# One load moved from SyncE's queue to ScalarE's, ahead of the row of parameters

## The chip, the cores and the metric

The kernel runs on one core of a Trainium2 chip. The metric is device time in microseconds (us) of one execution. Before the change it is 157.71 us, the median of 3 runs (157.62 to 158.26).

Engines are called by the profile's names: PE (TensorE, matrix products), PEld (its weight loads), DVE (VectorE), ACT (ScalarE), POOL (GpSimd), SP (SyncE, which here only issues DMAs). ACTq and SPq are the instruction queues of ACT and SP where they issue DMAs. Each engine works through its own queue in order.

## The reference

One block of a gated network on x (4 batches, 512 tokens, 512 features, float32), with a context of 4 x 512 tokens of 128 features:

```python
# attention part: W is [1, 256], ctx is [4, 512, 128]
si = ctx @ W[0, :128];  sj = ctx @ W[0, 128:]              # [4, 512] each
xij = sigmoid(si[:, :, None] + sj[:, None, :] + b)
x = x + tanh(g_xattn) * (0.6 * xij + 0.4 * layernorm(x))
# feed-forward part, all three products with quantized operands
h = layernorm(x)
x = x + tanh(g_ffn) * bitlinear(silu(bitlinear(h, w1)) * bitlinear(h, w2), w3)
```

`bitlinear(x, w)` normalizes x by its root mean square, rounds it to 8 bits with a scale per token, rounds w to -1, 0 or 1 after division by the mean of |w|, and multiplies. w1 and w2 are [1408, 512], w3 is [512, 1408].

## The kernel before

The 2048 tokens are 16 tiles of 128 tokens (4 tiles a batch). The context comes in transposed, 128 features on the partitions, 512 tokens of one batch in a block of 256 KB (`ctx_0` to `ctx_3`). x comes in tiles of 128 x 512 (256 KB).

The order of the work is written out by hand in `ORDER`, a list of steps; a table `STEPS` maps each step's name to a function, a loop at the end calls them in that order, and each engine gets its instructions in that order. Steps that matter here:

- `x0`, `x3`, ...: load a tile of x, on SP's queue (L133). `ctx0` to `ctx3`: load a block of the context, on SP's queue, by `load_ctx` (L139). `w1.0` and so on: load a part of a weight, on SP's queue (L144 for w1 and w2, L150 and L155 for w3).
- Ahead of the list: ACT's queue loads the row of attention weights `w_att` (1 KB, on one partition, into the tile `row`, L109), then the three scalars g_xattn, b_att and g_ffn into the same tile (`load_param`, L113). Then ACT runs one activation on the tile `warm` (L171), in front of which its function table is loaded.
- PE runs three filler products (`keep_busy`, L180, tile `idle`), then two products that turn the row into a column and into 128 equal rows (L185, L186, tile `bc`); ACT copies these to `wc` (L188).
- `bp1`, `up1`, `bp0`, `up0`: spread a scalar over the partitions on PE (L196) and take it up on ACT (L202, L204).
- `pi0`, `pj0`: the scores of batch 0 from `wc` and `ctx_0`, on PE (L315, L322). `si0` and `th`: bias and tanh on ACT (L327, L338). `st`, `at`: statistics of x and the gated sum, on DVE (L345, L366).
- `wu4`, `wu13`: 4 or 13 more filler products. `pi1`, `pj1`, `pi2` and so on: scores of the other batches.
- `A1.0a` ... `A1.4v`: sums of |w1| over parts, on ACT (a) or DVE (v). `tot1`: their total over the partitions, on PE (L248). `M1`: mean and its inverse, on DVE (L253 to L256). `R`, `C`: rounding and clipping of a weight (L264 to L269). `G`, `U`: the products with w1 and w2 (L459). `D`: the product with w3 (L526).

PE's queue therefore begins: three fillers, bc, bp1, bp0, pi0, pj0, pi1, four fillers, bp2, pj1, thirteen fillers, pi2, tot1. SP's queue begins: x0, ctx0, x3, x2, x1, ctx1, four parts of w1, ctx2, ctx3, four parts of w2.

Of the kernel before, what the change touches and what calls it, by code (L numbers as in the profile page):

```python
# [30 lines left out]
PACK, WORD = 4, F32  # L31

ORDER = """
x0 ctx0 x3 x2 x1 ctx1 w1.0 w1.1 w1.2 w1.3 ctx2 ctx3 w2.0 w2.1 w2.2 w2.3 x10 w3.0 x4 x6 x8 w3.1 w3.2
x14 x12 st0 bp1 up1 cg cc st3 bp0 up0 pi0 si0 st2 pj0 th2 st1 la2 th0 la0 th1 pi1 lb2v at2 si1 lb0v
at0 ce0v at1 ce1v am0 an0 th3 at3 am1 an1 A1.0a A1.1a A1.2a wu4 bp2 pj1 up2 wu13 pi2 A1.3v pjs1 sq1
A1.4v si2 ce3p sq0 am3 tot1 M1 ce2p r1p r0p pt1 un1a R1.2v pt0 un0v R1.3a am2 an3 pi3 si3 an2 C1.3v
C1.2v A2.0a th7 pj2 R1.0p C1.0v A2.1a wu4 G0.0 R1.1p A2.2v A2.3a C1.1v A2.4v G1.0 G1.1 st10 tot2 M2
R2.0v G0.1 r2v sq3 sq2 r3p G0.2 G0.3 dq0 C2.0v R2.1p st11 st5 C2.1v pjs2 R2.2a C2.2v pt3 pj3 SI0
# [23 lines left out]
def flamingo_gated_kernel(  # L63
# [16 lines left out]
    C = ctx_t.shape[0]  # L80
# [12 lines left out]
    act, dve, pool, pe, sp = nc.scalar, nc.vector, nc.gpsimd, nc.tensor, nc.sync  # L93
# [12 lines left out]


    row = const.tile([1, 2 * C + 3], F32, name="row")
    act.dma_start(row[:, : 2 * C], w_att)  # L109

    def load_param(i):
        src = (b_att, g_x, g_f)[i]
        act.dma_start(row[:, 2 * C + i : 2 * C + i + 1], src.rearrange("(o n) -> o n", o=1))  # L113
# [24 lines left out]
    def load_ctx(eng, b):  # L138
        eng.dma_start(ctxs[b], ctx_t[:, b * S : (b + 1) * S])  # L139

    def load_w(eng, i, k):
# [3 lines left out]
        else:  # L145
# [8 lines left out]
            if f1 > full:  # L154
# [2 lines left out]
                    w3t[HF:, :].rearrange("(p j) d -> p j d", j=REST),  # L157
                )

    for i in (1, 0, 2):  # L160
        load_param(i)

# [140 lines left out]
    am1 = const.tile(NTT, F32, name="am1")  # L303
# [315 lines left out]
```

## Time and profile before

| what | value |
|---|---|
| median of 3 runs | 157.71 us |
| the profiled execution, its own time | 157.83 us |
| its span, first to last instruction | 156.1 us |
| mean granted TensorE clock | 0.989 |
| PE busy | 146.2 us (94% of the span) |
| DVE busy | 126.9 us (81%) |
| ACT busy | 118.6 us (76%) |
| POOL busy | 97.4 us (62%) |
| loaded and stored | 18.21 MB |

The span is what the profile sees; the time of the execution has some 1.7 us around it. Busy shares are means over the whole span, which has a load stage, a long stretch in which PE is full, and a tail, and they say little of the first microseconds, where the change lies. For these one reads the timeline (each line: start, duration, engine, source line, operation, tiles written and read, how many in a row, and the idle time before with what ended it) and the chain of waits (the work that ended last, followed back from the end). A row of the windows view gives, for one stretch of time, its length, the busy time and number of instructions of PE, PEld, DVE, ACT and POOL, the granted clock, the share of the DMA engines and the GB/s. A row of the waits gives who waited for whom, the total in us, how often, and the longest.

### The profile page before, as it was taken

Reading aid. Unit: us, or ns where it says so; the run is one execution under the profiler, and the core shown is the slowest. Engines: PE = TensorE matmul, PEld = TensorE weight load, DVE = VectorE, ACT = ScalarE, POOL = GpSimd, SP = SyncE. Lnnn points to the kernel's source line nnn. Section 1 sums busy time; section 2 is a strip of 40 time slices with the busy share of each in tenths; the row PEclk is TensorE's granted clock in tenths of the full one; section 3 lists DMA queues with packets and bytes.
Section 4 is the critical chain, followed back from the end, with each engine's and each line's share of the span. In section 5 each row is a group of like instructions: output and inputs, shape, how many; then the busy total and the mean of one; then the engine's idle time right before and its main releaser. Section 6 shows DMA issues by size and latency. Waiting matters only on the chain.

```text
span 156.1 us, 2167 instructions
## 1 busy us (share of the span) xinstructions
PE 146.2 (94%) x704; PEld 75.4 (48%) x704; DVE 126.9 (81%) x216; ACT 118.6 (76%) x164; POOL 97.4 (62%) x161
## 2 busy tenths in 40 slices
PE   5999969979999999999999999999999999999980
PEld 2853643535554545555455454545554545555330
DVE  1679599999999999999999999959699296748621
ACT  3269499999799999997999879689979583737300
POOL 6241569782366886589959888889998962130400
PEclk9999995999999999999999999999999999999999
DMA  4799999996000000000000000100600321010162
GB/s 118 278 425 412 432 411 421 422 404 249 1 0 0 6 0 0 0 0 0 0 4 0 0 0 0 69 4 0 247 24 0 123 79 70 1 67 0 64 249 90
DMA packets 6690, 18.21 MB, mean 117 GB/s; under 512 B 663, under 2 KB 664, under 8 KB 6424
## 3 DMA queue, kind: packets, MB, share of 16 engines
q1 hardware_dynamic: 6672, 18.09, 29.4%
q8 instruction: 5, 0.08, 0.2%
q14 instruction: 5, 0.04, 0.1%
q10 hardware_dynamic: 8, 0.00, 0.0%
HBM read 13.89 MB, written 4.19 MB: 116 GB/s over the span
## 4 chain that ended last, share of the span: by engine, by line
PE 68%; DVE 21%; ACT 3%; POOL 3%; issue 1%; DVEq 0%; POOLq 0%; ACTq 0%
PE pg L459 19%; PE pu L459 18%; PE po L526 15%; PE idle L180 5%; DVE hs L471 5%; DVE f_am L483 5%; PE pj L322 3%; PE pi L315 3%; DVE x L366 2%; PE qp L419 2%; DVE x L531 2%; DVE am L388 2%; ACT junk L396 1%; DVE q L411 1%; PE pt L419 1%
## 5 line engine op out<-in xcount | busy, mean ns | idle before, releaser
L459 PEld LDWEIGHTS <-ht 128*128 128x128 f16 x384 | 37.7, 99 | 38.5 <-issue 3.5
L459 PE MATMUL pu<-w2q,ht 128*128 128x512 f16 (+1 forms) x192 | 40.4, 362 | 1.1 <-DVE w2q L269 1.1
L459 PE MATMUL pg<-w1q,ht 128*128 128x512 f16 (+1 forms) x192 | 41.1, 367 | 0.0
L526 PE MATMUL po<-w3q,qt 128*128 128x512 f16 x176 | 39.4, 379 | 0.7 <-ACT ht L427 0.4
L471 DVE SCALAR_TENSOR_TENSOR hs<-pu,a,hs 128x1408 f32<-128x1408 f32 x16 | 26.8, 1676 | 6.3 <-PE pu L459 2.4
L427 ACT ACTIVATE qt<-qp 128x1536 f16<-128x1536 int8 x14 | 20.2, 1448 | 12.9 <-PE qp L419 12.7
L526 PEld LDWEIGHTS <-qt 128*128 128x128 f16 x176 | 17.2, 98 | 20.1 <-issue 1.0
L467 ACT ACTIVATE hs<-pg,a 128x1408 f32<-128x1408 f32 x16 | 22.8, 1426 | 4.5 <-POOL a L406 2.4
L483 DVE TENSOR_REDUCE f_am<-hs 128x1 f32<-128x1409 f32 x16 | 25.7, 1609 | 0.1
L491 ACT ACTIVATE junk<-hs 128x1408 bf16<-128x1408 f32 x16 | 22.0, 1375 | 0.1
L500 POOL TENSOR_SCALAR q<-hs,f_qs 128x1024 int8<-128x1024 f32 (+1 forms) x22 | 19.2, 888 | 1.1 <-DVE f_qs L488 0.6
L531 DVE SCALAR_TENSOR_TENSOR x<-po,f_dq,x 128x512 f32<-128x512 f32 x16 | 11.9, 746 | 9.7 <-PE po L526 8.4
L345 DVE BATCH_NORM_STATS2 st<-x 128x6 f32<-128x512 f32 x16 | 10.8, 675 | 3.1 <-DMA x<-in_x_dram 3.1
L382 POOL TENSOR_SCALAR th_all<-x,ysum 128x512 f32<-128x512 f32 x9 | 6.8, 761 | 10.1 <-DVE x L366 6.6
L366 DVE SCALAR_TENSOR_TENSOR x<-x,sc,th_all 128x512 f32<-128x512 f32 x16 | 12.3, 788 | 0.7 <-ACT th_all L338 0.3
L411 POOL TENSOR_SCALAR q<-th_all,qs 128x512 int8<-128x512 f32 x15 | 10.3, 689 | 3.3 <-PE pt L419 1.4
L374 POOL TENSOR_SCALAR x<-x,c_sig,sh 128x512 f32<-128x512 f32 x14 | 11.6, 833 | 0.1
L516 POOL TENSOR_SCALAR f_w<-f_ss,kap 128x2 f32<-128x2 f32 (+1 forms) x9 | 2.4, 268 | 14.2 <-ACT junk L491 13.6
L388 DVE TENSOR_REDUCE am<-th_all 128x1 f32<-128x513 f32 x16 | 10.8, 676 | 0.0
L180 PE MATMUL idle<-ones 128*128 128x512 f16 x24 | 9.0, 534 | 1.8 <-POOL ones L175 1.8
L396 ACT ACTIVATE junk<-th_all 128x512 bf16<-128x512 f32 x16 | 10.1, 628 | 0.7
L427 ACT ACTIVATE ht<-pt 128x512 f16<-128x512 int8 x15 | 8.8, 589 | 1.9 <-PE pt L419 1.8
(94 smaller groups left out, 182.1 us busy)
## 6 DMA issues: line engine op xcount, KB each, us to landing
out_dram<-x SPq DMA_DIRECT2D x16, 256.0 KB, 2.3
x<-in_x_dram SPq DMA_DIRECT2D x6, 512.0 KB, 13.1
hs<-in_w1t_dram SPq DMA_DIRECT2D x4, 704.0 KB, 6.7
hs<-in_w2t_dram SPq DMA_DIRECT2D x4, 704.0 KB, 11.6
w3f<-in_w3t_dram SPq DMA_DIRECT2D x2, 1024.0 KB, 14.9
x<-in_x_dram SPq DMA_DIRECT2D x4, 256.0 KB, 5.1
ctx<-in_ctx_t_dram SPq DMA_DIRECT2D x4, 256.0 KB, 7.3
w3f<-in_w3t_dram SPq DMA_DIRECT2D x1, 768.0 KB
```

The costliest lines, as they stand in the source:

```text
L180: pe.matmul(idle[:, :512], ones16[:, :P], ones16, start=True, stop=True)
L366: dve.scalar_tensor_tensor(xt(n), xt(n), col(sc, n), ths[n], ALU.mult, ALU.add, accum_out=col(ysum, n))
L388: dve.tensor_reduce(col(am1, n), th_all[:, th_slot[n], : D + 1], AX.X, ALU.max, apply_absolute_value=True)
L427: act.activation(dst, src, AF.Copy)
L459: pe.matmul(gus[tag, n][:, c0 : c0 + cn], hts[n][:, kk, :], wq[:, kk, c0 : c0 + cn], start=(kk == 0), stop=(kk == ND - 1),)
L467: act.activation(tts[n], gus.pop(("pg", n))[:, :H], AF.Silu, scale=col(a1, n))
L471: dve.scalar_tensor_tensor(tts[n], gus.pop(("pu", n))[:, :H], col(a1, n), tts[n], ALU.mult, ALU.mult)
L483: dve.tensor_reduce(col(f_am, n), hs[:, t_slot[n], : H + 1], AX.X, ALU.max, apply_absolute_value=True)
L491: act.activation(junk[:, :H], tts[n], AF.Square, accum_out=col(f_ss, n))
L500: eng.tensor_scalar(dst, src, col(f_qs, n), 127.0, ALU.mult, ALU.mult)
L526: pe.matmul(po[:, :D], qt[:, f, :], w3q[:, f, :], start=(f == 0), stop=(f == NH - 1))
L531: dve.scalar_tensor_tensor(xt(n), pos.pop(n)[:, :D], col(f_dq, n), xt(n), ALU.mult, ALU.add)
```

## The change

The step `ctx0` is taken out of `ORDER`, so SP's queue goes from x0 straight to x3. In its place ACT's queue loads the first block of the context, by the same `load_ctx`, as its first DMA; the load of `w_att` now comes behind it, then the three scalars as before. Sizes, tiles and all other steps stay.

```diff
 ORDER = """
-x0 ctx0 x3 x2 x1 ctx1 w1.0 w1.1 w1.2 w1.3 ctx2 ctx3 w2.0 w2.1 w2.2 w2.3 x10 w3.0 x4 x6 x8 w3.1 w3.2
+x0 x3 x2 x1 ctx1 w1.0 w1.1 w1.2 w1.3 ctx2 ctx3 w2.0 w2.1 w2.2 w2.3 x10 w3.0 x4 x6 x8 w3.1 w3.2 x14
...
     row = const.tile([1, 2 * C + 3], F32, name="row")
-    act.dma_start(row[:, : 2 * C], w_att)
 
     def load_param(i):
...
+    load_ctx(act, 0)
+    act.dma_start(row[:, : 2 * C], w_att)
     for i in (1, 0, 2):
         load_param(i)
```

More of the change, by code (lines that the diff above doesn't have):

```diff
@@ L33 @@
 ORDER = """
-x0 ctx0 x3 x2 x1 ctx1 w1.0 w1.1 w1.2 w1.3 ctx2 ctx3 w2.0 w2.1 w2.2 w2.3 x10 w3.0 x4 x6 x8 w3.1 w3.2
-x14 x12 st0 bp1 up1 cg cc st3 bp0 up0 pi0 si0 st2 pj0 th2 st1 la2 th0 la0 th1 pi1 lb2v at2 si1 lb0v
-at0 ce0v at1 ce1v am0 an0 th3 at3 am1 an1 A1.0a A1.1a A1.2a wu4 bp2 pj1 up2 wu13 pi2 A1.3v pjs1 sq1
+x0 x3 x2 x1 ctx1 w1.0 w1.1 w1.2 w1.3 ctx2 ctx3 w2.0 w2.1 w2.2 w2.3 x10 w3.0 x4 x6 x8 w3.1 w3.2 x14
+x12 st0 bp1 up1 cg cc st3 bp0 up0 pi0 si0 st2 pj0 th2 st1 la2 th0 la0 th1 pi1 lb2v at2 si1 lb0v at0
+ce0v at1 ce1v am0 an0 th3 at3 am1 an1 A1.0a A1.1a A1.2a wu4 bp2 pj1 up2 wu13 pi2 A1.3v pjs1 sq1
 A1.4v si2 ce3p sq0 am3 tot1 M1 ce2p r1p r0p pt1 un1a R1.2v pt0 un0v R1.3a am2 an3 pi3 si3 an2 C1.3v
```

## The prediction

> **What bounds the kernel now.** I read the page first, for which engine fills which stretch, then the chain of waits, for what the first 20 us hang on, then the timeline of that stretch, then the waits of DVE and of the SP queue.
>
> The page's 40 slices (3.9 us each) have the granted clock and the DMA rate:
>
> ```profile
> PEclk9999995999999999999999999999999999999999
> DMA  4799999996000000000000000100600321010162
> GB/s 118 278 425 412 432 411 421 422 404 249 1 0 0 6 0 0 0 0 0 0 4 0 0 0 0 69 4 0 247 24 0 123 79 70 1 67 0 64 249 90
> ```
>
> The loads stream at about 420 GB/s from 8 us to 35 us; the first two slices are well below that. The chain of waits (start us, us, what) begins so:
>
> ```profile
> 1.82 1.46 PE idle L180 x3
> 3.28 0.51 PE bc L185 x2
> 3.80 0.65 PE bc L186 x2
> 4.45 0.02 issue
> 4.47 0.29 ACT wc L188
> 4.76 0.04 issue
> 4.80 0.58 PE spread L196 x2
> 5.38 0.10 issue
> 5.49 1.84 PE pi L315 x8
> 7.32 1.92 PE pj L322 x2
> ...
> 14.98 3.62 PE idle L180 x13
> 18.60 0.80 PE pi L315 x8
> ```
>
> See that PE never stands for a DMA here: the row's first matmul (L185) starts when the three fillers end, and everything up to 18.6 us is one unbroken queue on PE. DVE's waits between 8 and 36 us say what this queue holds up:
>
> ```profile
> DVE mean L253 <- PE tot L248: 1.7, 1, 1.7
> ```
>
> DVE stands 1.7 us, until 19.65, for the total of w1, which sits on PE behind that queue; its own last input for it was done at 17.4. From 19.65 to 28.0 DVE works without a gap (M1, rounding, clipping, M2), PE then waits 1.1 us for w2q (L269, 33.6), and from 33.6 PE is full. So a delay of PE's first instructions is a delay of M1, and I see no cover for it behind M1.
>
> The timeline of the start (start us, us, what):
>
> ```profile
> 0.72 0.51 ACTq L109 DMA_DIRECT2D row<-in_w_att_dram  x1
> 0.72 0.20 POOL masks.py:197 MEMSET ident<- 128x128 f32 x1 [0.29 <-POOLq L599]
> 0.72 0.38 SPq L133 DMA_DIRECT2D x<-in_x_dram  x1
> ...
> 1.16 0.42 SPq L139 DMA_DIRECT2D ctx<-in_ctx_t_dram  x1
> ...
> 1.27 0.21 ACTq L113 DMA_DIRECT2D row<-in_g_xattn_dram  x1
> ```
>
> The trace's records of semaphores and packets, which the page only sums up, say when these landed: row 1.96, x0 3.36, g_x 3.42, b 4.05, g_f 4.23, ctx0 5.35, x3 6.70. What PE wants of them: row at 3.21 (slack 1.25), g_x at 4.23 for bp1 (0.8), b at 4.80 for bp0 (0.75), ctx0 at about 5.3 for pi0, which starts at 5.46, 0.11 after ctx0 landed. So ctx0 costs 0.1 us at most today. Its landing is late for a reason: the windows view has
>
> ```profile
> 3.50:5.00 1.50, 1.35 (x7) 1.26 (x7) 0.87 (x3) 0.48 (x3) 0.00 (x0) 1.00 0.26 71
> ```
>
> 71 GB/s between 3.5 and 5.0 us, after 269 in the 1.5 us before, with ctx0 and x3 both issued. I don't know what stalls there.
>
> **The change, part by part.**
>
> *SP loses one issue.* 0.42 us of SP (1.16 to 1.58); x3 and x2 are issued that much earlier. Worth nothing on the chain: the only wait for these in the stretch is DVE's 0.7 us for x3 at 6.7, and DVE has 1.7 us to spare before M1. Were that cover gone, it would be worth 0.4 us.
>
> *ACT gains one issue in front of four.* Nearest rows: 0.33 to 0.42 for a ctx block on SP, 0.51 for ACT's first issue. I take 0.45, so row, g_x, b, g_f and the table load (2.09, 1.28 us) all start 0.4 to 0.5 later. ACT's first consumer, wc, starts at 4.47 after 0.9 us of idling, so the table load is covered; without that idling it would cost the 0.45.
>
> *The row now queues behind 256 KB.* This is the term that counts. The row has one partition, and its records are one 1024-byte packet (0.044 us) and one 4-byte one, on one DMA engine. In the trace of before, that engine worked off the small and the large transfers in turn: row at 1.62, eight x0 packets of 2 KB, g_x at 2.88, eight ctx0 packets until 3.53, then b and g_f at 3.54 and 3.56. So 2-KB packets ahead do delay a 4-byte one: g_x took 2.2 us from issue to landing, against 1.24 for the row. After the change row, g_x, b and g_f stand in ACT's own queue behind ctx0's eight packets, with x0's eight running beside them. Those 16 packets took until 3.53 before; I take the same. Row packet at 3.55, landing 0.3 (row) to 0.5 (g_x, b) later: 3.95. PE's L185 then starts at about 4.0 instead of 3.21: +0.8. Bounds: if ACT's packets all go ahead of x0's, ctx0's share ends near 2.9 (as x0's did) and the row lands at 3.3, +0.1; if the row is caught in the stalled stretch and lands only when ctx0 did, 5.35, it is +2.2. Landings of g_x and b right behind the row (4.1 to 4.2) stay within their wanted times, which move too (5.0 and 5.6). From the +0.8 the 0.1 us that pi0 stood for ctx0 comes off: **+0.7 at pi0**.
>
> The Trainium skill, page "DMA: Bandwidth & Descriptors", section "Issuing engines are not separate DMA queues", speaks against the change: DMAs issued from several engines run on the same 16 DMA engines and interleave, so a second issuer saves only the sequencer's time. By that rule the gain is the 0.42 us of SP above, which nothing waits for, and the sum stays positive; the order in which the trace shows engine 0 serving both queues agrees.
>
> *SP's later issues.* The SP queue waits for earlier transfers:
>
> ```profile
> SPq L144 <- DMA ctx<-in_ctx_t_dram: 1.2, 1, 1.2
> SPq L599 <- PEq L599: 0.7, 1, 0.7
> SPq L139 <- DMA x<-in_x_dram: 0.6, 2, 0.3
> ```
>
> The trace has eight landing semaphores in turn; a ninth transfer waits for the first. Today x1 (2.59) waits for the row, ctx1 (3.38) for x0, w1.0 for g_x, w1.1 (5.37) for ctx0. With ctx0 first in line, x1 probably waits for ctx0 or x0: issued at 3.4 to 3.9, some 1 us later, with ctx1, w1.0 and the rest queued behind it. Ahead of them x0, ctx0, x3 and x2 are 1 MB, 2.5 us at 420 GB/s, so the engines have work until about 4.8, and x1's first packet comes about 1 us after its issue (x0: 0.72 to 1.75). I cost it at nothing. Cover: pi1 starts at 8.71 and ctx1 landed at 8.60; with PE 0.7 later ctx1 may land at 9.3. If it comes later, each us costs PE a us.
>
> *What of +0.7 reaches the end.* The next thing on PE that isn't paid in work is the clock. Four fillers at 10.60 took 1.87 us (0.43 apart); of the 13 from 14.78 the first four start 0.43 apart and the rest 0.216. The clock records show full rate from 16.49 to 23.32, half to 26.73, then full again: steps of 3.41 us. If the step at 16.49 stays where it is, PE's fillers begin at 15.48, only 2.4 of them run slow instead of 4, and the queue's end moves by 0.35 and not by 0.7. If the step moves with the work or by chance, all 0.7 pass. I take the middle, **+0.5**. The skill's page "TensorE: Matmul & The Clock Gate", Part 1, says that the window is free-running and doesn't restart with the kernel; by it the 0.35 of one execution is not a rule, and the mean would be 0.7. The 3.41 us spacing agrees with its figure.
>
> Sum: 157.83 (the profiled execution; span 156.1 and 1.7 around it) + 0.5 = 158.3; it stands 0.12 above the median 157.71, which gives **158.2**.
>
> **The rivals.**
>
> *No difference: the row is not late.* The engines may serve ctx0 on ACT first and the row at 2.9. Then pi0 gains its 0.1: 157.6. Against: x0 and ctx0 start in the same 0.1 us and the first packets take 0.26 to 0.4 us each.
>
> *Slower, clearly: the stall takes the row.* If the row's read is caught in what held the engines at 71 GB/s, it lands between 4.7 and 5.35, PE starts 1.5 to 2.2 later and, with half to all of it passed on, the time is 158.5 to 159.8; middle 159.2. It decides from a landing of about 4.4 on. For it: ctx0 itself took 4.2 us. Against: b and g_f passed at 3.54.
>
> *Slower by the clock.* If the window that ends at 16.49 isn't busy enough any more, the nine fast fillers cost 0.21 more each: +1.9, 159.6 or so. PE's wait of 0.8 lies at 3.3, far from it.
>
> *Faster: the stall disappears.* With ctx0 and x0 abreast the 1.5 us at 71 GB/s may be filled, and the whole stream come up to 1.2 us earlier. The one place where the chain touches data in the first 36 us is ctx0 (0.1), so a gain needs a DMA wait that the view hides, or a clock step to its favour: 156.9 at best guess. Against: DVE had A1.3v's data at 15.49 and still stood for PE, and w3.1 landed at 35.11 for a use at 35.94.
>
> **How the numbers follow.** 0.5% (0.79 us) is about what a measurement of this kernel can tell. Row late by 0.3 to 1.1: 0.50, giving 157.9 to 158.8, of which 0.19 lies above 158.50 (all 0.7 or more passed on, or the row later than I take it) and 0.31 below. No difference: 0.15. Stall takes the row: 0.18, all above. Clock: 0.07, above. Faster: 0.10, below 156.92. So slower 0.19 + 0.18 + 0.07 = 0.44, same 0.31 + 0.15 = 0.46, faster 0.10. The range goes from 157.1 (leaving out most of the faster case) to 159.5 (leaving out half of the clock's and the top of the stall's).
>
> **What would show it.** Right: ACTq issues ctx0 at 0.72 and the row at 1.2; L185 starts at about 4.0 with an idle gap on PE ended by the row's DMA; pi0 at 6.1 to 6.2 with ctx0 landed long before; DVE's wait for tot stays near 1.3 to 1.7, since its own work before it waits for pj0 and moves too, and ends at 20.0 to 20.4 instead of 19.65; everything from M1 on is shifted alike. Wrong: L185 still at 3.2, or at 5 and later; pi0 waiting for ctx0; pi1 waiting for ctx1; a clock step at another place than 16.5.

## The result, and the profile after

The changed kernel takes 158.69 us (median of 11 runs, 158.22 to 159.80) beside 157.62 us for the kernel before (11 runs, 156.65 to 158.88). The ratio is 1.0085, 95% interval 1.0057 to 1.0113: slower by 0.85%. Run again beside other kernels it was 1.0065 (1.0038 to 1.0092). A ratio leaves out a run that lies more than 1.5% above the fastest of its kernel; in all that follows this is one run of the version with fewer fillers. The profiled execution took 158.40 us, its span is 156.6 us. Code lines are one higher after the change (L185 is L186, L459 is L460), and L133, L139 and L144 are now L132, L138 and L143.

The timeline of the first five microseconds after the change, with lines left out:

```profile
0.72 0.40 ACTq L138 DMA_DIRECT2D ctx<-in_ctx_t_dram  x1
...
0.72 4.68 SPq L132 DMA_DIRECT2D x<-in_x_dram  x4
...
1.15 0.54 ACTq L160 DMA_DIRECT2D row<-in_w_att_dram  x1
...
4.85 0.55 PE L186 MATMUL bc<-ones,row 1*128 1x1 f32 x2 [1.56 <-DMA row<-in_w_att_dram]
4.91 0.69 DVE L346 BATCH_NORM_STATS2 st<-x 128x6 f32<-128x512 f32 x1 [3.91 <-DMA x<-in_x_dram]
```

PE now stands 1.56 us for the row, which landed at 4.71 (before: 1.96), and the first product of the row comes at 4.85 instead of 3.21. DVE stands for x0, too, which landed at 4.88 instead of 3.36. And ctx0, the transfer that the change puts first, landed at 5.06 instead of 5.35: issued 0.44 us earlier, it came 0.29 us earlier. The SP line says more: its four loads of x tiles take 4.68 us together, because the fourth, x1, is not issued before 5.07. The waits of SP in the first 9 us, after the change:

```profile
SPq L132 <- DMA ctx<-in_ctx_t_dram: 3.0, 1, 3.0
SPq L600 <- PEq L600: 0.7, 1, 0.7
```

So SP stood 3.0 us for ctx0. Everything behind x1 on its queue moved: ctx1 landed at 10.21 (before 8.60), the last part of w1 at 17.18 (15.49), the last of w2 at 26.45 (23.67). The chain of waits no longer begins with PE's fillers; its start, to 26 us:

```profile
...
0.72 4.34 DMA ctx<-in_ctx_t_dram
5.06 0.02 issue
5.07 0.33 SPq L132
5.40 0.04 issue
5.45 0.43 SPq L138
5.88 0.04 issue
5.92 6.01 DMA hs<-in_w1t_dram
11.94 0.02 issue
11.95 12.82 DMA hs<-in_w2t_dram
24.77 0.02 issue
24.79 1.62 DVE acc L245
...
```

It runs through ctx0's landing, SP's held issue, the weights, and into DVE's sum over a part of w2 (step A2.2v), which waits for its data. Before, no DMA stood in the first 30 us of this chain. DVE's waits between 8 and 36 us say the same in small:

```profile
DVE x L367 <- ACT th_all L339: 0.9, 1, 0.9
DVE mean L254 <- PE tot L249: 0.8, 1, 0.8
...
DVE acc L245 <- DMA hs<-in_w2t_dram: 0.3, 1, 0.3
```

The wait for w1's total, 1.7 us before, is 0.8, although M1 comes later (20.31 instead of 19.65): DVE's own work before it ended at 19.47 instead of 17.96, so later by more. M2 comes at 28.54 instead of 27.96, and from there on nothing differs: the span ends 128.1 us behind M2 in both.

### The profile page after: what moved, and what is told of

The parts are those of the page before. It is cut to its first block, busy times and chain, and to the rows that moved or that the text cites. A ratio compares the mean times of both kernels' runs of the same rounds, so it can differ in the third digit from the quotient of the medians.

```text
span 156.6 us, 2167 instructions
## 1 busy us (share of the span) xinstructions
PE 145.3 (93%) x704; PEld 75.0 (48%) x704; DVE 126.6 (81%) x216; ACT 118.4 (76%) x164; POOL 97.4 (62%) x161
## 3 DMA queue, kind: packets, MB, share of 16 engines
HBM read 13.89 MB, written 4.19 MB: 115 GB/s over the span
## 4 chain that ended last, share of the span: by engine, by line
PE 53%; DVE 24%; DMA 15%; POOL 3%; ACT 1%; issue 1%; SPq 0%; DVEq 0%; ACTq 0%
PE pu L460 18%; PE pg L460 17%; PE po L527 15%; DMA hs<-in_w2t_dram 8%; DVE hs L472 5%; DVE f_am L484 5%; DMA hs<-in_w1t_dram 4%; DMA ctx<-in_ctx_t_dram 3%; DVE x L367 2%; PE qp L420 2%; DVE x L532 2%; DVE am L389 2%; DVE acc L245 2%; DVE st L346 1%; DVE q L412 1%
## 5 line engine op out<-in xcount | busy, mean ns | idle before, releaser
L460 PEld LDWEIGHTS <-ht 128*128 128x128 f16 x384 | 37.5, 98 | 37.7 <-issue 2.2
L460 PE MATMUL pu<-w2q,ht 128*128 128x512 f16 (+1 forms) x192 | 40.4, 361 | 1.1 <-DVE w2q L270 1.1
L460 PE MATMUL pg<-w1q,ht 128*128 128x512 f16 (+1 forms) x192 | 40.3, 361 | 0.0
L181 PE MATMUL idle<-ones 128*128 128x512 f16 x24 | 8.0, 480 | 1.8 <-POOL ones L176 1.8
```

The lines of the kernel that those rows point to most:

```text
L460: pe.matmul(gus[tag, n][:, c0 : c0 + cn], hts[n][:, kk, :], wq[:, kk, c0 : c0 + cn], start=(kk == 0), stop=(kk == ND - 1),)
```

## The experiments

Two theories. *The row*: it lands late behind ctx0, PE starts late, M1 and all behind it move. *The held queue*: x1 and what stands behind it on SP wait for ctx0, so ctx1 and the weights come late. A third thing had to be watched, the step of PE's clock, whose place I couldn't predict.

This table has, for each profile, the times in us of the row's first product on PE, of pi0, of ctx1's landing, of pi1 and pj1 on PE, of the clock's step to full rate, of M1 and M2, and the span less M2. All are read from the timelines and the trace's records of landings and clock.

| kernel | row on PE | pi0 | ctx1 landed | pi1 | pj1 | clock step | M1 | M2 | span - M2 |
|---|---|---|---|---|---|---|---|---|---|
| before | 3.21 | 5.49 | 8.60 | 9.03 | 12.91 | 16.49 | 19.65 | 27.96 | 128.1 |
| before_look1 | 3.21 | 5.52 | 8.99 | 9.12 | 13.13 | 14.28 | 18.67 | 26.84 | 128.1 |
| before_look2 | 3.21 | 5.32 | 8.67 | 8.89 | 12.81 | 14.01 | 18.37 | 26.56 | 128.1 |
| after | 4.85 | 6.92 | 10.21 | 10.49 | 14.37 | 15.89 | 20.31 | 28.54 | 128.1 |
| after_again | 4.80 | 6.87 | 10.32 | 10.46 | 14.47 | 16.08 | 20.32 | 28.52 | 128.1 |
| hold_x1 | 3.21 | 5.41 | 10.38 | 10.51 | 14.52 | 17.81 | 21.11 | 29.42 | 128.0 |
| late_row_free_sp | 3.62 | 5.69 | 9.93 | 10.07 | 14.08 | 16.96 | 20.47 | 28.78 | 128.1 |
| row_ctx_par | 3.20 | 6.82 | 7.63 | 10.39 | 14.27 | 17.76 | 20.96 | 29.27 | 128.1 |
| row_on_sp | 4.37 | 6.43 | 8.67 | 10.01 | 13.89 | 15.41 | 19.61 | 27.87 | 128.1 |
| hold_row | 10.43 | 12.49 | 8.49 | 16.07 | 19.95 | 23.35 | 26.59 | 34.91 | 128.0 |
| row_par_ctx | 3.21 | 8.34 | 9.29 | 11.89 | 15.76 | 18.40 | 22.03 | 30.34 | 128.1 |
| wu8 | 3.21 | 6.82 | 9.28 | 10.37 | 14.24 | 15.68 | 19.25 | 27.58 | 128.1 |
| ctx0_first | 3.21 | 5.40 | 10.00 | 10.14 | 14.15 | 18.48 | 21.26 | 29.57 | 128.1 |
| ctx0_first_wu8 | 3.21 | 5.39 | 9.92 | 10.06 | 14.07 | 15.93 | 19.24 | 28.55 | 128.0 |

The last column is the reading that carries the rest: in fourteen profiles, over a range of 8 us, the end comes 128.0 to 128.1 us behind M2. What a change does ahead of M2 passes to the end one to one, and in none of these versions did a later load count.

**The changed kernel again.** No edit.

> The changed kernel once more, beside the next three on the same chip. Both theories take it as it was: ratio to before near 1.0085, the row's first matmul (L186) near 4.8 us, x1 issued on SP near 5.1 us.

Ratio 1.0065 (1.0038 to 1.0092); x1 issued at 5.40, the row on PE at 4.80, M1 at 20.32 as in the first profile (20.31). But M1 is not held up by the same thing. DVE's waits between 8 and 36 us, cut to one line:

```profile
DVE acc L245 <- DMA hs<-in_w1t_dram: 0.9, 1, 0.9
```

Here DVE stands 0.9 us for the last part of w1, which landed at 18.07 (17.18 in the first profile), and has no wait for PE's total of w1, which is done at 20.28; DVE turns to it at 20.32. So the held queue reaches M1 by a way that doesn't lead over PE: the landing of w1's last part and 2.25 us of DVE's work behind it. Before the change that sum would be 15.49 + 2.25 = 17.74, 1.9 us ahead of M1.

**Hold SP's queue, leave the row.** In the kernel before:

```diff
+    pool.tensor_copy(xs[0][:, 1, 0:1], wc[:, 0:1])
     for step in ORDER.split():
```

> The kernel before, with one POOL copy of a column of wc into the place of x1 ahead of its load, so that SP cannot issue x1 (nor what is queued behind it) before wc is there, about 5.0 us instead of 2.6; the row stays early. The theory that the late row costs the time expects no difference, ratio 0.998 to 1.002, with M1 at 19.6 to 19.8. The rival, that the held-up SP queue and the later load stream cost it, expects w2's last part 1 to 2 us later than 23.7, DVE or ACT waiting for w2, and a ratio of 1.004 to 1.009.

Ratio 1.0098 (1.0062 to 1.0134). The theory of the row alone falls here: the row is as early as before, pi0 starts at 5.41, and the kernel is as slow as the changed one. The waits of its first 12 us and of SP's first 8 us:

```profile
PE pi L315 <- DMA ctx<-in_ctx_t_dram: 1.3, 1, 1.3
```

```profile
SPq L133 <- POOL x L571: 2.4, 1, 2.4
```

SP stands 2.4 us, ctx1 lands at 10.38, and PE stands 1.3 us for it ahead of pi1, which starts at 10.51, where it starts in the changed kernel too (10.49). DVE's wait isn't for w2, as the expectation had it: it stands 2.4 us for w1's last part (landed at 18.10) and then 0.7 for PE's total.

**Keep the row late, free SP.** In the changed kernel:

```diff
-    def load_param(i):
+    def load_param(i, eng=act):
         src = (b_att, g_x, g_f)[i]
-        act.dma_start(row[:, 2 * C + i : 2 * C + i + 1], src.rearrange("(o n) -> o n", o=1))
+        eng.dma_start(row[:, 2 * C + i : 2 * C + i + 1], src.rearrange("(o n) -> o n", o=1))
...
+    load_param(1, sp)
     load_ctx(act, 0)
     act.dma_start(row[:, : 2 * C], w_att)
-    for i in (1, 0, 2):
+    for i in (0, 2):
         load_param(i)
```

> The changed kernel with only g_xattn's load moved to the head of SP's queue, so that x1 on SP waits for that small transfer instead of ctx0; the row still stands behind ctx0 on ACT's queue. The theory of the late row expects L186 at 4.0 to 5.0 us, as in the changed kernel, and a ratio of 1.004 to 1.009. The rival of the held-up SP queue expects a ratio of 0.998 to 1.002, since x1 is issued near 2.6 us again.

Ratio 1.0072 (1.0037 to 1.0106), but the edit did not do what it was meant to. x1 still waited for ctx0 (2.7 us on SP, issued at 5.21), and the row landed at 3.49, so PE lost only 0.4 us by it. It is a second case of a held queue with an almost punctual row: PE stands 0.6 us for ctx1 ahead of pi1 at 10.07, and DVE 1.1 us for w1's last part. It speaks against the row alone, too, and does not test what it was built for.

**Row first, then ctx0, then the scalars, on ACT.** In the changed kernel:

```diff
-    load_ctx(act, 0)
     act.dma_start(row[:, : 2 * C], w_att)
+    load_ctx(act, 0)
```

> The changed kernel with the row's load put back as ACT's first, ctx0 behind it and then the scalars: one part of the change undone, ctx0 stays on ACT's queue. Both theories expect the row to land near 2.0 us, x1 to be issued near 2.6 us again and a ratio of 0.997 to 1.002. If the two queues side by side are themselves the cost (contention of ctx0 with x0), the ratio stays above 1.004. The scalars now stand behind ctx0: if b or g_xattn lands after 5 us, pi0 starts later than 5.5 for that reason.

Ratio 1.0073 (1.0042 to 1.0104); both theories expected none. The row landed at 1.95, x1 was issued at 2.08 and ctx1 landed at 7.63, the earliest of all. But the scalars now stood behind ctx0, and the waits of the first 12 us say what that does:

```profile
PE spread L197 <- DMA row<-in_g_xattn_dram: 1.5, 1, 1.5
```

PE stands 1.5 us for g_xattn, which landed at 5.83 instead of 3.42; pi0 started at 6.82, and pi1 at 10.39 with its data there since 7.63. SP's queue was not quite free: it stood 2.1 us for ctx0 ahead of w1's first part, yet w1 landed as before (its last part at 15.45, before 15.49), and w2's third part at 23.25, 6.0 us ahead of M2. So a late start of PE alone also gives the loss. What is late need not be the row: here it is another small transfer behind ctx0. The third case of the expectation, ctx0 and x0 in each other's way, has this number too, but PE waits for neither: x0 landed at 3.22 and ctx0 at 5.65, ahead of g_xattn.

**Move only the row, behind x0 and ctx0 on SP.** In the kernel before:

```diff
-    act.dma_start(row[:, : 2 * C], w_att)
...
     for i in (1, 0, 2):
         load_param(i)
+    load_x(0, 1)
+    load_ctx(sp, 0)
+    sp.dma_start(row[:, : 2 * C], w_att)
```

with x0 and ctx0 taken out of `ORDER`.

> The kernel before, with only the row's load moved: from the head of ACT's queue to SP's queue behind x0 and ctx0. ctx0 stays on SP, and x1 waits for a small early transfer, so SP is not held. By the order in which the engine served the queues before, the row's packet comes at 3.55 us and lands at 3.9 to 4.1. The theory that PE's start sets M1 expects L185's successor (the row's first product) at 4.0 to 4.2 us, pj1 0.6 to 0.9 later than 12.9, M1 later by that or by half of it, depending on where the clock step falls, and a ratio of 1.001 to 1.007. The rival that only the held SP queue counts expects M1 unmoved and a ratio of 0.998 to 1.001.

Ratio 1.0022 (0.9997 to 1.0047). The row landed at 4.23, its product came at 4.37, PE stood 1.1 us, and pj1 was 1.0 later than before, all a little above what was expected. M1 at 19.61 is no later than in the first profile of before, because the clock's step fell at 15.41 here, ahead of the fillers (2.97 us instead of 3.82). The time moved the expected way, by 0.35 us, which the interval (0.74 at most) separates neither from none nor from much of the 1.0 us: this run doesn't decide between the theories.

**Hold the row long.** In the kernel before, the load of the row is taken from its place and issued behind a memset on POOL (the lines of q8 are moved up from below):

```diff
-    act.dma_start(row[:, : 2 * C], w_att)
...
     pool.memset(ones16, 1.0)
+    QS, q_slot = 3, itertools.count()
+    q8 = const.tile([P, QS, NQ * P], I8, name="q8")
+    pool.memset(q8[:, :, HF:], 0)
+    pool.memset(row[:, 0:1], 0.0)
+    act.dma_start(row[:, : 2 * C], w_att)
...
-    QS, q_slot = 3, itertools.count()
-    q8 = const.tile([P, QS, NQ * P], I8, name="q8")
-    pool.memset(q8[:, :, HF:], 0)
```

> The lateness of the row doubled: the kernel before, with the row's load held by a POOL memset into the row and by the landing of ctx0, so that it is issued on ACT near 5.4 us and lands near 6.7. SP's queue and ctx0 are as before. The theory of PE's start expects the row's first product near 6.8 us (3.6 later than before), pj1 near 16.4, M1 near 22.3 if the fillers all run at full clock, and a ratio of 1.014 to 1.023. The rival of the SP queue expects at most 1.003.

Ratio 1.0442 (1.0413 to 1.0471). The memset was done at 3.11; the row, whose turn it was to wait for ctx0 (landed at 5.46), was issued at 5.54, as meant, and landed not at 6.7 but at 10.29: 4.75 us for 1 KB, with the parts of w1 under way on SP's queue. PE stood 7.15 us. So the delay was twice the one intended, and it passed whole: pj1 7.0 us later, M1 6.9, M2 7.0, the span 6.9. The row's path alone can set the end, with SP's queue as before.

**ctx0 on ACT's queue behind row and scalars.** In the changed kernel:

```diff
-    load_ctx(act, 0)
     act.dma_start(row[:, : 2 * C], w_att)
     for i in (1, 0, 2):
         load_param(i)
+    load_ctx(act, 0)
```

> ctx0 on ACT's queue behind the row and the three scalars: both suspected costs of the change are gone, the move itself stays. The row lands at 2.0 us, the scalars by 3.5, ctx0 at 5.0 to 5.6, x1 is issued near 2.6 and ctx1 lands at 7.5 to 8.6. Both theories expect pi0 at 5.3 to 5.8 and a ratio of 0.997 to 1.002; if the move itself costs through two large transfers side by side, 1.004 or more.

Ratio 1.0128 (1.0099 to 1.0158), worse than the changed kernel and outside what either theory expected; by the number it is the third case, in which the move itself costs. The row and the scalars are about as early as before, and SP issues x1, ctx1 and w1 about as early. But ctx0, issued at 2.11 behind x0, x3, x2 and x1 of the other queue, landed at 8.21:

```profile
8.34 1.84 PE L316 MATMUL pi<-wc,ctx 128*128 128x1 f32 x8 [2.95 <-DMA ctx<-in_ctx_t_dram]
```

Now pi0 itself stands 2.95 us. That queue order costs more than the change did. Whether ctx0 lost this time as the fifth in line or because large transfers ran side by side, the run doesn't say.

**Fewer fillers.** In the kernel before:

```diff
-at0 ce0v at1 ce1v am0 an0 th3 at3 am1 an1 A1.0a A1.1a A1.2a wu4 bp2 pj1 up2 wu13 pi2 A1.3v pjs1 sq1
+at0 ce0v at1 ce1v am0 an0 th3 at3 am1 an1 A1.0a A1.1a A1.2a wu4 bp2 pj1 up2 wu8 pi2 A1.3v pjs1 sq1
```

> The kernel before with 8 instead of 13 filler products ahead of pi2 (wu8 for wu13); nothing else. The theory that M1's time, set by PE's queue, passes to the end one to one expects pi2, tot1 and M1 about 1.1 us earlier (M1 at 18.5 to 18.8, DVE is ready at 18.0) and a ratio of 0.991 to 0.996. If something else than M1 sets the end, the ratio stays within 0.998 to 1.002; if the clock falls to half in the stretch for want of fillers, M1 gains nothing and the ratio is 1.000 to 1.010.

Ratio 0.9919 (0.9889 to 0.9949): 156.75 us beside 158.03. This is the version that beats both kernels. In its profile ctx0 happened to land at 6.68, pi0 at 6.82, and M1 still came at 19.25 and M2 0.4 earlier than in the first profile of before. The gain is what the shortened queue ahead of M1 would give (1.1 us by five fillers at 0.216); the gain by the ratio is 1.3 us. One of its six runs took 158.93 us, at a mean granted clock of 0.978 where the others had 0.989 to 0.994; the last experiment comes back to that.

**The kernel before, profiled twice more.**

> The kernel before, unchanged, profiled again. ctx0 landed at 5.0 to 5.5 us in most profiles that leave its load alone, but at 6.7 in wu8, which has the same loads. If that landing is a matter of chance, another profile of the same kernel gives another value between 5 and 7, pi0 follows it 0.1 us behind, and the clock's step falls at another place than 16.49. If both are fixed for this kernel, 5.35 and 16.49 come back within 0.1.

> The same once more, for the same question: two values of ctx0's landing and of the clock's step beside the first profile's 5.35 and 16.49.

Times 156.72 and 156.42 us. ctx0 landed at 5.38 and 5.18 and pi0 started within 0.2 us of the first profile, so that part came back. The clock's step did not: 14.28 and 14.01 instead of 16.49. M1 came 1.0 and 1.3 us earlier by it, and the time followed. PE's part of the timeline from 12 us on, in the first profile of before, then in before_look2:

```profile
12.91 2.08 PE L322 MATMUL pj<-ctx,wc 128*128 128x512 f32 x2
14.78 3.82 PE L180 MATMUL idle<-ones 128*128 128x512 f16 x13
18.43 0.95 PE L315 MATMUL pi<-wc,ctx 128*128 128x1 f32 x8
```

```profile
12.81 1.70 PE L322 MATMUL pj<-ctx,wc 128*128 128x512 f32 x2
14.35 2.97 PE L180 MATMUL idle<-ones 128*128 128x512 f16 x13
17.16 0.95 PE L315 MATMUL pi<-wc,ctx 128*128 128x1 f32 x8
```

pj starts within 0.1 us of the same place; the thirteen fillers take 2.97 us instead of 3.82, since the step to full rate came ahead of them, and the products behind them start 1.27 us earlier. The same kernel, and as much as the change is worth. In the changed kernel's profile the step came ahead of the fillers too:

```profile
14.37 1.87 PE L323 MATMUL pj<-ctx,wc 128*128 128x512 f32 x2
16.07 2.97 PE L181 MATMUL idle<-ones 128*128 128x512 f16 x13
19.03 1.02 PE L316 MATMUL pi<-wc,ctx 128*128 128x1 f32 x8
```

So the two profiles can't be set against each other without the clock. From 14.37 against 12.91 the change has 1.46 us of lateness ahead of the fillers, and 0.60 behind them: 0.86 was given back by the fillers, which is a matter of where the step fell. Against before_look2, with the step ahead of the fillers in both, the lateness is 1.56 us at pj and 1.87 at the products. The ratio from many runs, 1.0 to 1.3 us, is the better measure of the change than any pair of profiles.

**ctx0 first, on SP's own queue.** In the kernel before, the line of `ORDER` that SP works off:

```diff
-x0 ctx0 x3 x2 x1 ctx1 w1.0 w1.1 w1.2 w1.3 ctx2 ctx3 w2.0 w2.1 w2.2 w2.3 x10 w3.0 x4 x6 x8 w3.1 w3.2
+ctx0 x0 x3 x2 x1 ctx1 w1.0 w1.1 w1.2 w1.3 ctx2 ctx3 w2.0 w2.1 w2.2 w2.3 x10 w3.0 x4 x6 x8 w3.1 w3.2
```

> The aim of the change by another way: ctx0 ahead of x0 on SP's own queue, the row first on ACT as before. ctx0 lands near 3.3 us, where x0 landed before, and x0 near 5.3. If what hurts is the row's and the scalars' place, and ctx0's own landing costs the kernel before only 0.1 us, the ratio is 0.997 to 1.001, with pi0 at 5.3 to 5.5. If ctx0's landing varies and costs the kernel before more on average, 0.992 to 0.997. If x0 is missed more than ctx0, 1.002 or more, with DVE's first gate constants behind x0.

Ratio 1.0081 (1.0051 to 1.0110). The row is as early as before (1.96), no scalar is waited for (b landed at 4.63 instead of 4.05), no queue is changed but by the exchange of two neighbours, and the time is that of the changed kernel. The wait came, though not where the expectation put it. SP's waits of the first 8 us, and PE's second start of pi in the timeline:

```profile
SPq L139 <- DMA ctx<-in_ctx_t_dram: 2.2, 1, 2.2
```

```profile
5.40 1.84 PE L315 MATMUL pi<-wc,ctx 128*128 128x1 f32 x8
7.10 2.05 PE L322 MATMUL pj<-ctx,wc 128*128 128x512 f32 x2
10.14 1.84 PE L315 MATMUL pi<-wc,ctx 128*128 128x1 f32 x8 [0.98 <-DMA ctx<-in_ctx_t_dram]
```

ctx0, issued at 0.72 as the first of its queue, landed at 5.26; as the second, at 1.16, it had landed at 5.35. The issue of ctx1, whose turn it now is to wait for ctx0 instead of x0, stands 2.2 us; ctx1 lands at 10.00 and PE stands 1.0 us for it. This is the held queue with a punctual row once more, and without a POOL instruction put in.

**ctx0 first, with fewer fillers.** Both edits:

```diff
-x0 ctx0 x3 x2 x1 ctx1 w1.0 w1.1 w1.2 w1.3 ctx2 ctx3 w2.0 w2.1 w2.2 w2.3 x10 w3.0 x4 x6 x8 w3.1 w3.2
+ctx0 x0 x3 x2 x1 ctx1 w1.0 w1.1 w1.2 w1.3 ctx2 ctx3 w2.0 w2.1 w2.2 w2.3 x10 w3.0 x4 x6 x8 w3.1 w3.2
...
-at0 ce0v at1 ce1v am0 an0 th3 at3 am1 an1 A1.0a A1.1a A1.2a wu4 bp2 pj1 up2 wu13 pi2 A1.3v pjs1 sq1
+at0 ce0v at1 ce1v am0 an0 th3 at3 am1 an1 A1.0a A1.1a A1.2a wu4 bp2 pj1 up2 wu8 pi2 A1.3v pjs1 sq1
```

> ctx0 ahead of x0 on SP and 8 fillers for 13 together. If both act on PE's queue ahead of M1 and DVE is ready at 18.0, M1 comes at 18.4 to 19.0 and the ratio is 0.987 to 0.993, the end 136.3 to 136.5 us behind M1 as in every profile so far. If the fillers are missed by the clock, M1 is at 19.5 or later.

Ratio 1.0054 (1.0015 to 1.0092): most of the gain of wu8 is gone. In the profile PE's queue did get shorter, M1 comes at 19.24 as in wu8, though here DVE has no wait for PE's total and w1's last part sets M1 (landed at 17.00, M1 2.24 later). But M2 comes 9.3 us behind it, where all other profiles have 8.2 to 8.3. DVE's waits between 8 and 36 us:

```profile
DVE acc L244 <- DMA hs<-in_w2t_dram: 1.3, 1, 1.3
```

The sum A2.2v stands 1.3 us for the third part of w2, which landed at 24.74, 3.8 us ahead of M2; in the changed kernel's profile it landed at 24.77, 3.8 ahead of M2, and DVE stood 0.3; in wu8's, where ctx0 came late by chance, at 23.80, 3.8 ahead of M2, and DVE stood 0.4. So M2 is the later of two things, M1 + 8.2 to 8.3, and the landing of that part + 3.8. With SP's queue held, the second forms a floor: 24.77 + 3.8 is 28.57, within 0.05 us of M2 of the changed kernel, and M1 + 8.2 to 8.3 comes there too. In that profile PE being earlier would be worth nothing more. The landing varies between runs, and much of the loss is something else: five of the twelve runs took 159.3 to 159.8 us at a mean clock of 0.978, the other seven 157.45 to 158.40 (median 157.56, beside 157.65 before) at 0.987 to 0.993. Half rate for one more step of 3.41 us would be 1.7 us, or 0.011 of the span's mean clock, which is what these five lack. That eight fillers at times leave PE too idle for the clock would fit, but no run at 0.978 has a profile: the 1.7 us are an estimate from the spacing of the steps, and the cause is not shown.

## Why the prediction was right or wrong, point by point

The time, 158.69, lies in the range (157.1 to 159.5) and 0.5 above the forecast of 158.2. The likeliest case by its sign, within 0.5%, did not come: the kernel is slower by 0.65 to 0.85%, to which I gave 0.44 against 0.46. That the time still came so near owes something to luck: two terms of the sum were too small, and they meet at one point, where only the larger counts.

**The row.** Right in kind: it lands behind ctx0, PE stands for it, and nothing but PE's own lateness is seen at pj1. Wrong in size. The step that failed is "Those 16 packets took until 3.53 before; I take the same". The row's packet, which I put at 3.55, came at 4.11 and took another 0.6 to land (I took 0.3, and 3.55 + 0.3 is 3.85, or 3.89 with the packet's 0.04, not my 3.95): 4.71 instead of 3.95, PE +1.6 instead of +0.8, pi0 +1.43 instead of +0.7. The trace doesn't name the engine of a packet; which packets shared the row's engine I inferred from the order of their times. This is the low end of the rival in which the stall takes the row. The windows of the two kernels from 2.50 to 3.25 us (stretch, its length, busy time of PE, PEld, DVE, ACT and POOL, granted clock, DMA share, GB/s), before, then after:

```profile
2.50:3.25 0.75, 0.75 (x3) 0.04 (x1) 0.00 (x0) 0.75 (x1) 0.58 (x1) 1.00 0.86 325
```

```profile
2.50:3.25 0.75, 0.75 (x2) 0.00 (x0) 0.00 (x0) 0.66 (x1) 0.58 (x1) 1.00 0.46 93
```

Where the engines had moved 325 GB/s for x0, they moved 93. The slow stretch that I had seen at 3.5 to 5.0 us lies earlier here, and in ctx0_first too, where ctx0 is also issued at 0.72 (97 GB/s from 2.25 to 3.5). I had read it as a place in time. It may go with the reading of ctx0, but in row_ctx_par, with ctx0 issued at 1.26, 236 GB/s moved from 3.5 to 5.0. What makes it, no run settled.

**ctx0 and pi0.** I took 0.1 us off for ctx0's earlier landing. With pi0 at 6.92 ctx0 is long there, and from the second spread to pi0 it takes 0.51 us (from 6.41) instead of 0.69 (from 4.80): some 0.2 came off, which is why pi0 is late by 1.43 and the row's product by 1.64. The term was right, and small.

**SP's later issues.** "I cost it at nothing" failed. I had named the mechanism, x1 waiting for ctx0 through the semaphores in turn, and its price, a us of PE for each us by which ctx1 is later than 9.3. But I put x1's issue at 3.4 to 3.9, which fits x0's landing of before (3.36), though I had named ctx0 or x0 as what it would probably wait for, and ctx0 had landed at 5.35. It was 5.07, SP stood 3.0 us, and ctx1 landed at 10.21. With the row as I had it (pi0 at 6.2), PE would have come to pi1 at 6.2 + 3.54 = 9.7, and ctx1 at 10.21 would have cost another half us. Beyond what I thought of, the whole stream of weights comes 1.6 to 2.8 us later and puts a floor under M1 (w1's last part + 2.25, which sets it in the second profile) and one under M2.

**Row or queue?** Both, and a late start of PE or a held queue is enough by itself. hold_x1 and ctx0_first have the punctual row and the held queue: 1.0098 and 1.0081. row_ctx_par has ctx1 early and a late PE: 1.0073. The row itself, late with a free queue, was run only by 1.1 us (row_on_sp, not clear of none) and by 7.15 (hold_row, passed whole), so that its 1.6 us alone would give the whole loss is argued from these and not shown. In the changed kernel the two put pi1 at the same place: pi1 followed pi0 by 3.54 us before, so PE, late by the row, gets to it at about 6.92 + 3.54 = 10.46, and ctx1 lands at 10.21. PE has no wait for ctx1 there. Further on they stay as close: in the first profile PE's total sets M1 and the third part of w2 holds DVE 0.3 us ahead of M2, in the second DVE, late by w1, and PE's total reach M1 within 0.1 us. With both there the cost is the larger of the two and not their sum, and so can't be divided between them.

**The clock.** I took the middle between 0.35 and 0.7 for what gets past the fillers. In the profile of after 0.66 of 1.46 arrived at M1, but not for the reason given, a step that stays where it is: it fell at 15.89 instead of 16.49, and in before alone it falls at 14.0, 14.3 and 16.5. Set against the work it is steadier: in all fourteen profiles, hold_row's included, it comes 5.1 to 8.3 us after pi1's start, a spread of 3.2 us and so within one of the clock's steps of 3.41. It moves with PE's work, and its place within a step changes from one execution to the next. By the Trainium skill, page "TensorE: Matmul & The Clock Gate", Part 1, the window runs freely and doesn't restart with the kernel; the three profiles of before agree with that. By that rule the whole lateness passes in the mean. Measured over many runs are 1.0 to 1.3 us at the end, for 1.46 at pj1 in the profile. Not every version passes it whole: row_par_ctx, 2.85 us later at pj1, took 2.0 us more (1.6 to 2.5), and row_on_sp, 1.0 later, 0.35 (at most 0.74); what kept back the rest stays open.

**What was right.** No cover behind M1: the span less M2 is 128.0 to 128.1 in all fourteen profiles. ACT's table load stayed hidden: it ran from 2.59 to 3.87, and wc began at 6.07. SP's saved 0.42 us bought nothing. The skill's page "DMA: Bandwidth & Descriptors", section "Issuing engines are not separate DMA queues", says that a second issuer saves only the sequencer's time; the runs agree (SP saved 0.42 us, and nothing came of it). They add that the move changes what stands behind what, and the cost came from there.

**The rivals.** "The row is not late" and "the stall disappears" fell, by row 4.71 and by a stream that comes later. "Slower by the clock" wasn't seen in the changed kernel: its fillers ran at full rate, and its runs have a mean clock of 0.987 to 0.989, as those of before beside the repeat; a loss of that kind showed only with eight fillers. "The stall takes the row" came, at its low end, with a second cause beside it that I had dismissed.

## What to carry to other kernels

Before a large transfer is moved ahead, list the small ones that then stand behind it on its queue, and the later issues whose turn it is to wait for its landing; put its landing where the trace has it and not where its place in the line would let one hope. Find the last point to which all paths add up (here M2, 128 us ahead of the end) and read every experiment there, because two delays that meet at one point cost the larger and not the sum. And look at one kernel several times before a difference of a microsecond between two profiles is read as the change: here the place of the clock's step alone moved M1 by 1.3 us.

## What the runs showed of the hardware that I had not expected

ctx0's landing hardly depends on whether it is issued first or second. Issued at 0.72, on ACT's queue or on SP's, it landed at 5.06 to 5.38; issued second on SP at 1.16, at 5.03 to 5.46, once at 6.68; second on ACT at 1.26, at 5.65. Only as the fifth large transfer, at 2.11, was it clearly later, at 8.21. What the 0.44 us of an earlier issue bought doesn't stand out from this spread.

A transfer of 1 KB can take 4.75 us: in hold_row the row went out at 5.54 beside parts of w1 of 704 KB and landed at 10.29. The same row as the first transfer of its queue takes 1.24.

The clock's step to full rate falls anywhere between 14.0 and 18.5 us in these fourteen profiles (hold_row, whose PE is 7 us late, aside), between 14.0 and 16.5 in one unchanged kernel, where it moves M1 by 1.3 us. It is the one cause that its three profiles show for the spread between its runs; wu8, in which ctx0 landed at 6.68 with the same loads, hints at a second.
